# Turned tiles through DRAM in one transfer each way, larger pieces, Wqkv in parts, and a new order: a stack of four graph layers

## The chip, the cores and the metric

The kernel runs on one core of a Trainium2 chip. That core has TensorE (PE, matrix products into PSUM banks), VectorE (DVE), ScalarE (ACT), GpSimd (POOL) and SyncE (SP, which here only issues transfers), and 16 DMA engines that all issuing queues share. The metric is the device time of one execution in microseconds (us); lower is better. Times are medians over several executions. The profile is of one more execution.

## The reference

64 graphs of 256 nodes with 256 features pass through four layers. Each layer is followed by a residual and a normalisation without weights. Cut to what matters:

```python
# layer 0: transformer block over allowed = adj | adj.T | eye
q, k, v = split(x @ Wqkv.T + bqkv)            # 8 heads of 32
attn = softmax(where(allowed, q * scale @ k.T, -inf))
x1 = layernorm(x + (attn @ v) @ Wo.T + bo)
y = layernorm(x1 + relu(x1 @ W1.T + b1) @ W2.T + b2)
x = norm(x + y)
# layers 1 and 2: graph attention
h = x @ W.T                                    # layer 2: x @ W, no bias
e = leaky_relu(f[:, None] + g[None, :])        # f = h @ a1, g = h @ a2
x = norm(x + softmax(where(adj > 0, e, -big)) @ h + bias)   # layer 2: elu
# layer 3: two relation convolutions with mask adj == 1
h = elu(x @ w_root + (mask.T @ x / deg) @ w_rel + b)        # twice
x = norm(x + h)
```

All of it is float32. The second relation (`adj == 1` and `adj != 1`) is always empty.

## The kernel before

Everything for one graph is held as tiles of 128 partitions: 256 nodes are `NB` = 2 blocks of 128 nodes, 256 features are `KB` = 2 blocks of 128 features. A graph goes through some 60 operations. A small planner, `Plan`, receives all operations of all 64 graphs (`plan.op`: engine, planned cost, tiles read and written), and `schedule` decides the order in which each engine gets them. It walks through planned time. On each engine it takes, of the first 40 waiting operations, the ready one with the smallest due date. A due date is an entry of the table `DUE` (one per kind of operation) plus the graph's entry in `LATER`. Tiles live in rings of fixed size (`RINGS`: four `T`, one `turned`, one `blocks`, eight PSUM banks and so on); an operation waits until a buffer of its ring is free. The planned time matters only for the order: on the chip each engine runs its list, and semaphores do the waiting. Many graphs are in flight at once. TensorE changes between full products ("full"), scores in four row strips ("row", `L852`), values in four column strips ("col", `L873` and `L878`), single-pass gathers ("one", `L1036`) and transposes ("bits", "turn", "spread"); the planner counts a cost for a change of mode.

A matrix product needs its left operand with features on partitions. Where an activation has nodes on partitions it must be turned. Five times per graph (ahead of the feed-forward, of both graph attentions and of both convolutions) `bounced` does this without TensorE, for all but the last `QUICK` = 5 graphs: VectorE transposes 32x32 blocks (`L730`), SyncE sends the result to a DRAM tile `rows` in four transfers (`L734`, one for each 32 partitions, pieces of 128 bytes), then reads it back as `T` in one (`L737`, 2 KB per partition). The last five graphs go through ScalarE and TensorE instead (`L720`, `L709`, `L712`). The graph attention needs the column f on all partitions: VectorE transposes it (`L927`), SyncE writes it to DRAM (`L930`, `row<-cols`) and reads it back to all partitions (`L932`, `pf<-row`); then VectorE adds g and the mask (`L962`), applies the slope (`L965`), ScalarE takes the exponent (`L967`) and TensorE multiplies (`bank<-h,e`, in `product`, `L758`). The input x is read in eight strided transfers of 32-column blocks (`L748`) and transposed on VectorE (`L751`). SyncE carries all of these in one queue, with the loads of adj, x, xr, the weights and the output; a transfer that waits for its source holds up all that stand behind it.

At the start, GpSimd issues the loads of the small rows and columns (biases, norm weights) in program order, ahead of the planned part, and SyncE loads the weights as planned operations; Wqkv is one transfer of 768 KB (`L603`). GpSimd also computes the reciprocal root for each normalisation (`L772` to `L775`) and adds residuals with accumulating transfers (`L694`).

Of the kernel before, what the change touches and what calls it, by code (L numbers as in the profile page):

```python
# [18 lines left out]
P = 128  # L19
# [8 lines left out]
SENT, BACK = 3.2, 5.5  # L28
SENT_ROW, BACK_ROW = 2.6, 4.0
# [8 lines left out]
WORTH = 0.0  # L38
DUE = [
    -174.49, -30.67, -218.4, -13.1, -273.08, -58.54, -61.59, 77.04, -149.86, 411.77, 271.23, -47, 251.55, 289.26, 409.16, 111.82, -128.45, 340.23, 45.84, 214.03,  # L40
    175.89, -1.19, 78.77, -279.42, -23.39, 48.71, -130.17, -271.08, 149.73, -13.73, -89.69, -232.88, 470.18, 336.16, 222.8, 97.87, -54.4, -162.22, 370.88, 259.56,
    78.73, 64.78, 119.93, 148.71, -8.47, 151.17, -563.4, 216.96, 420.85, 105.36, -12.18, -73.5, -248.72, -183.23, -128.19, -297.4, -582.46, -629.93, -428.77, -624.34,
    -537.46, -889.65, -508.26, -787.82, -567.19, -632.7, -195.48, -656.32, -574.02, -727.78, -913.06, -538.96, -358.22, -951.51, -201.95, -392.63, -228.91, -130.77, -538.26, -399.3,
    -375.81, -885.24, -308.54, -281.69, -300.68, -236.73, -468.35, -102.24, -553.09, -355.09, -301.16, -135.84, -203.16, -68.79, 262.12, -373.58, -588.44, -396.63, -287.4, -163.41,
    -84.14, -161.3, 55.46, -37.62, -225, -68.62, -53.45, -173.79, -244.33, -312.15, -25.06, -130.25, -229.38, -357.91, -210.44, -689.16, -856.94, -453.15, -790.88, -481.92,
    -836.21, -389.2, -777.71, -103.26, -3.29, -1145.93, -317.53, -276.38, -81.48, -574.66, -449.44, -205.39, -496.42, 24.49, -179.79, -136.43, -325.16, 317.31, -603.82, -343.72,
    -371.81, -548.18, -331.53, -31.09, -128.17, 130.86, 1.87, 511.93, 153.26, 401.39, 149.72, -317.69, -500.74, -300.47, -371.15, -311.4, -333.58, 113.13, -178.32, -161.32,
    -448.39, -246.01, -410.16, -80.08, 6.31, -309.66, 11.59, -465.92, -681.64, -971.69, -916.97, -1014.65, -1262.62, -1383.05, -948.84, -855.59, -947.76, -1379.9, -710.53, -943.35,
    -553.21, -1028.37, -899.15, -683.97, -671.33, -379.95, -374.5, -674.01, -484.29, -173.96, -190.22, 54.18, -383.06, 111.01, -316.54, -124.36, -70.55, -86.53, -531.14, 531.14,
    -183.27, 110.54, 117.46, 350.27, -72.47, 19.93, -141.94, 64.33, 75.75, -83.28, 27.66, 87.87, -121.34, -128.76, 173.68, 156.59, 237.41, -282.51, 244.56, 209.74,  # L50
    181.62, 154.65, 180.84, 257.31, 326.57, 204.39, -182.17, 95.7, -191.88, -185.24, -7.82, -360.89, -20.59, -54.79, -173.03, 30.75, 310.52, 55.03, -458.58, -368.62,
    -301.68, -425.9, -464.37, -637.73, -768.61, -334.28, -150.16, -409.84, -355.26, 122.24, -107.85, -228.07, 47.36, 408, -92.61, 15.96, 80.96, 138.89, 67.4, 142.09,
    158.28, 47.13, -505.17, -320.95, -173.93, 136.21, 121.43, -45.74, -24.76, 91.57, -290.1, 89.8, -77.57, -224.12, 192.91, -503.22, -155.9, -61.04, -122.6, -163.72,
    -107.28, -293.92, -129.55, -48.17, -73.67, -152.32, -47.67, -88.39, -67.35, -95.35, -1.39, -120.46, -71.97, -99.95, -99.2, -83.54, -273.5, -100.86, -98.97, -246.65,
    -114.52, -84.34, -84.04, 213.08, -101.14, 28.99, -107.58, -166.35, -71.43, -370.62, -85.77, -54.9, -39.02, -105.24, -132.96, -80, 5.5, -143.22, -204.86, -87.44,
    -263.61, -54.97, -36.69, -15.51, -150.63, -138.2, -82.22, -46.11, -96.06, -107.06, -98.34, 5.8, -77.33, -106.96, -77.26, -94.63, 22.37, 44.75, 10.33, 81.65,
    -68.87, -13.71, -8.74, 3.65, 15.2, 59.74, -109.39, -109.42, -109.88, -122.53, -153.4, 80.8, -115.07, -211.16, -102.09, 220.31, -109, -81.64, -158.53, -140.27,
    -107.57, -47.12, -22.07, -162.83, 48.73, 31.08, -70.41, 95.56, -407.18, -102.6, 47.72, 10.89, -50.86, -71.44, -51.48, -13.16, -277.35, -101.83, -6.3, -268.19,
    -222.87, -172.64, -189.41, -85.76, -139.13, -181.79, -197.93, -115.69, -157.05, -73.06, -49.75, -158.63, -59.31, -93.55, -49.94, -151.39, -107.24, -72.78, -174.55, -70.55,
    -115.83, -293.85, -133.83, -133.95, -53, -133.17, -282.53, -145.74, -78.83, -104.42, -92.18, -145.7, -18.49, -17.87, 15.35, 6.67, 13.62, 57.04, -67.96, -80.53,  # L60
    39.58, -194.32, -44.64, -60.96, 7.1, -78.89, -48.83, -228.02, -4.68, -206.89, -2.65, -161.5, -34.42, -254.75, -53.95, -243.38, -118.23, -87.33, -28.27, -75.81,
    -104.07, -131.73, -309.88, -25.6, -45.95, -54.93, -91.47, -65.34, -123.35, -297.34, -138.27, -184.68, -109.73, -213.04, -117.5, -106.99, -266.96, -100.44, -97.67, -251.87,
    -284.74, -134.37, -0.22, -92.93, -117.19, -149.69, -97.23, -240.05, -139.35, 23.43, -35.17, -258.95, -117.88, -48.18, 188.95, -46.24, -145.12, -208.04, -268.67, -473.43,
    -272.21, -243.87, -112.49, -128.6, -313.79, -205.48, -109.56, 37.28, 213.35, -231.44, -290.26, -289.71, -171.01, -132.76, -35.5, -66.35, -9.67, -136.84, 463.57, -61.18,
    184.12, -198.15, 1.05, -86.21, -198.53, 114.21, -45.3, 54.56, -158.67, 15.98, -107.93, -77.74, -220.68, -453.53, -169.7, -88.06, -73.23, 116.03, -78.79, -74.27,
    -101.78, -96.73, 110.02, -273.88, -179.48, 265.32, -56.81, -46.47, -337.24, 102.8, -39.43, -355.3, 48.47, -235.68, -149.28, -635.75, -184.62, -148.96, -91.93, -52.81,
    -4.66, -351.52, -80.82, -238.88, 120.91, 93.83, 36.33, -177.41, -8.05, -48.92, 237.79, 75.79, 57.38, 313.29, 416.04, -82.45, 107.24, 191.68, 210.97, 64.43,
    -95.28, 310.12, 119.46, 67.34, -56.8, 46.35, 349.66, -74.87, -121.91, 34.56, 85.3, -52.75, 171.82, -341.78, -100.06, 126.59, -3, -262.55, 252.68, -39.97,
    -34.25, 131.75, -115.25, -2.99, -197.27, 22.45, -320.1, -187.93, -292.11, -133.05, -160.27, -66.47, -287.97, -208.92, -255.29, -419.07, -250.78, -500.29, -419.05, -440.34,
    -214.95, -115.45, -269.74, -319.13, -164.13, 4.5, 312.76, 82.06, 197.79, -30.08, -107.1, -286.77, -202.4, -646.95, -623.59, -467.76, -559.5, -318.22, -579.06, -404.03,  # L70
    -240.35, -65.58, -45.1, -153.25, 0.49, -146.16, 126.66, -34.71, -1.62, -179.37, -139.47, 227.43, -132.26, -290.26, -155.39, -51.64, 302.94, 246.87, 140.96, 204.3,
    -104.02, 71.81, 8.99, -126.86, 146.56, 0.86, 224.19, -152.01, 446.31, 131.78, 368.32, 314, 696.06, 347.08, 48.35, 187.69, 15.42, 78.29, 465.97, 264.4,
    166.9, 290.74, 160.47, 408.01, 590.72, 239.64, 475.03, 380.34, 133.8, 687.34, 377.65, 308.54, 177.24, 65.33, 352.6, 314.21, 19.52, 347.97, 321.54, -336.83,
    3.98, -110.06, -47.03, -163.4, -245.48, -59.58, 115.24, 69.33, 372.47, -20.84, 150.47, 264.59, -12.21, 46.26, 54.33, -331.12, -185.97, 15, -146.62, -307.28,
    -254.98, -482.4, 152.73, -443.86, -412.27, -99.19, -430.71, -271.66, -293.58, -545.9, -437.17, -236.15, -421.41, -139.02, -460.75, -814, -498.15, -872.83, -740.21, -107.52,
    -228.09, -535.02, -395.02, -152.46, -87.71, 186.76, -37.36, 173.3, 81.12, 213.05, -123.34, 215.75, -164.1, 319.76, 149, -26.56, 205.77, -219.36, 37.38, -51.04,
    12.57, -45.81, -10.44, -181.5, -100.86, 192.74, -72.9, 46.38, 442.42, -123.26, -157.49, -248.77, -433.39, -229.01, -111.35, -158.81, -169, -125.94, -243.05, -250.7,
    -209.85, -296.59, -119.49, -584.47, -331.14, -426.1, -318.14, -619.25, -168.44, -92.39, -109.4, -4.46, -154.38, -381.47, -282.5, -508.95, -97.11, -110.59, -181.94, -319.69,
    -366.24, -15.54, -364.82, -456.16, -363.15, 9.73, -177.14, -241.89, -206.34, 62.66, -415.85, -255.33, 28.1, 30.17, -150.26, -285.39, -10.72, -64.69, -59.2, -351.31,
    -213.36, -348.36, -100.2, -532.45, -196.58, -289.33, -155.62, -288.87, -509.51, -208.57, -148.76, -328.27, -11.7, -356.16, -232.87, -88.94, -499.61, -524.58, -539.29, -354,  # L80
# [1269 lines left out]
```

## Time and profile before

| | us |
|---|---|
| median of 3 runs (lowest to highest) | 2803.42 (2802.26 to 2806.78) |
| the profiled execution, its time | 2808.35 |
| its span, first to last instruction | 2806.6 |
| TensorE busy | 2744.8 |
| VectorE busy | 2480.0 |
| ScalarE busy | 1580.3 |
| GpSimd busy | 851.8 |
| mean granted TensorE clock | 0.996 of full |

The page lists the engines' busy time, where the span is cut into 40 slices, the queues of the transfers, a chain of work followed back from the last instruction, and groups of instructions by source line. A float32 product appears as two records; the ends of matmul records are modelled, so that a busy TensorE can hide short waits. "PEld" are weight loads, which run beside products. A wait line names the waiting engine and line, whom it waited for, the total, how often, and the longest. "SPq" is SyncE's queue: the duration there is that of issuing a transfer, not of the transfer.

### The profile page before, as it was taken

To read this page: it belongs to the slowest core of one execution; us is meant where nothing else is said; L and a number is where in the kernel's file an instruction comes from. 1 tells how busy PE (TensorE), PEld (TensorE's weight loads), DVE (VectorE), ACT (ScalarE), POOL (GpSimd) and SP (SyncE) were. 2 spreads that over 40 slices of the span, in tenths; PEclk is the share of its full clock that TensorE was granted. 3 is DMA by queue.
4 is the path that set the end of the run, shared out by engine and by line. 5 is a ranking of instruction groups with operands and counts; after the bars stand their busy time and mean duration, and the time that the engine had idled before them with its cause. 6 is when DMAs were issued, how large, how long until landed. Compare 5 with 4: busy or idle time off the path is not lost.

```text
span 2806.6 us, 50451 instructions
## 1 busy us (share of the span) xinstructions
PE 2744.8 (98%) x15790; PEld 2082.0 (74%) x15790; DVE 2480.0 (88%) x6527; ACT 1580.3 (56%) x3827; POOL 851.8 (30%) x1753
## 2 busy tenths in 40 slices
PE   6999999999999999999999999999999999999997
PEld 5787777777777777767777777777777777777784
DVE  5788989898898988989889899899899998889877
ACT  3555565554555645646556556556555565556576
POOL 3232233332323323323233223323332232333232
PEclk9999999999999999999999999999999999999999
DMA  8455665655656656565665655766566655664221
GB/s 193 98 110 109 127 136 111 133 124 109 131 113 137 124 113 128 113 133 118 123 126 118 133 119 112 142 120 130 109 128 132 122 121 115 130 141 100 55 43 32
DMA packets 960073, 330.62 MB, mean 118 GB/s; under 512 B 780184, under 2 KB 913304, under 8 KB 959800
## 3 DMA queue, kind: packets, MB, share of 16 engines
q1 hardware_dynamic: 915240, 276.32, 44.5%
q0 software_dynamic: 44560, 51.01, 12.2%
q8 instruction: 128, 2.10, 0.3%
q14 instruction: 145, 1.19, 0.1%
HBM read 183.12 MB, written 94.23 MB: 99 GB/s over the span
## 4 chain that ended last, share of the span: by engine, by line
PE 65%; DVE 18%; DMA 8%; SPq 3%; ACT 3%; issue 2%; POOL 1%; DVEq 0%; POOLq 0%; ACTq 0%
PE bank L758 55%; DMA rows<-turned 3%; PE bank L852 3%; PE bank L878 3%; PE bank L1036 3%; SPq L734 2%; DMA o<-X 2%; PE bank L873 2%; DVE turned L730 2%; DVE p L860 2%; DMA pf<-row 1%; DVE inv L884 1%; DVE st L767 1%; DVE X L689 1%; DVE lo L1024 1%
## 5 line engine op out<-in xcount | busy, mean ns | idle before, releaser
L772 POOL TENSOR_SCALAR rstd<-mv 128x2 f32<-128x2 f32 x384 | 102.0, 266 | 1434.4 <-DVE mv L769 1098.2
L758 PE MATMUL bank<-cw,T 128*128 128x512 f32 x1024 | 471.0, 595 | 1.5 <-DMA T<-rows 0.8
L779 ACT ACTIVATE X<-X,rstd 128x256 f32<-128x256 f32 x640 | 349.1, 596 | 214.9 <-POOL rstd L775 207.4
L758 PE MATMUL bank<-T,w 128*128 128x256 f32 x2048 | 464.4, 380 | 0.8 <-DMA T<-rows 0.6
L758 PE MATMUL bank<-w,hid 128*128 128x256 f32 x2048 | 460.6, 380 | 0.0
L758 PEld LDWEIGHTS bank<-w,hid 128*128 128x128 f32 x2048 | 387.4, 190 | 62.2 <-issue 10.7
L758 PEld LDWEIGHTS bank<-T,w 128*128 128x128 f32 x2048 | 385.2, 190 | 61.4 <-issue 9.0
L858 ACT ACTIVATE p<-bank 128x512 f32<-128x512 f32 x512 | 300.1, 598 | 100.0 <-PE bank L852 99.6
L860 DVE TENSOR_TENSOR p<-p,am 128x512 f32<-128x512 f32 x512 | 332.2, 677 | 14.2 <-ACT p L858 12.7
L758 PEld LDWEIGHTS bank<-cw,T 128*128 128x128 f32 x1024 | 188.8, 190 | 180.1 <-issue 162.7
L773 POOL TENSOR_TENSOR rstd<-rstd,neghalf 128x2 f32<-128x2 f32 x384 | 301.6, 785 | 32.1
L913 ACT ACTIVATE hid<-bank,col_b 128x256 f32<-128x256 f32 x512 | 215.8, 471 | 137.7 <-PE bank L758 136.6
L758 PE MATMUL bank<-h,e 128*128 128x259 f32 x1024 | 251.2, 386 | 10.4 <-ACT e L967 10.3
L758 PE MATMUL bank<-xT,wqkv 128*128 128x256 f32 x1024 | 245.2, 386 | 7.8 <-DMA wqkv<-in_WqkvT_dram 7.1
L758 PE MATMUL bank<-gw,T 128*128 128x258 f32 x1024 | 246.8, 382 | 1.3 <-DVE X L896 1.1
L758 PEld LDWEIGHTS bank<-h,e 128*128 128x128 f32 x1024 | 192.3, 191 | 72.8 <-issue 22.4
L884 DVE RECIPROCAL inv<-bank 128x256 f32<-128x256 f32 x128 | 221.3, 1739 | 25.9 <-PE bank L878 25.7
L767 DVE BATCH_NORM_STATS2 st<-X 128x6 f32<-128x256 f32 x640 | 236.3, 410 | 2.0
L758 PEld LDWEIGHTS bank<-xT,wqkv 128*128 128x128 f32 x1024 | 193.7, 192 | 48.7 <-issue 20.7
L730 DVE STREAM_TRANSPOSE turned<-X 128x512 f32<-128x512 f32 x236 | 165.3, 700 | 65.5 <-DMA rows<-turned 52.2
L758 PEld LDWEIGHTS bank<-gw,T 128*128 128x128 f32 x1024 | 191.3, 190 | 34.6 <-issue 5.5
L1023 ACT CAST hi<-bank 128x256 fp32r<-128x256 f32 x256 | 94.5, 370 | 211.0 <-PE bank L758 210.6
(129 smaller groups left out, 4684.5 us busy)
## 6 DMA issues: line engine op xcount, KB each, us to landing
rows<-turned SPq DMA_DIRECT2D x1180, 64.0 KB
T<-rows SPq DMA_DIRECT2D x295, 256.0 KB
adj<-in_adj_dram SPq DMA_DIRECT2D x128, 256.0 KB
blocks<-in_x_dram SPq DMA_DIRECT2D x512, 32.0 KB
x<-in_x_dram SPq DMA_DIRECT2D x64, 256.0 KB
xr<-in_x_dram SPq DMA_DIRECT2D x64, 256.0 KB
xr<-row_ln_b POOLq DMA_DIRECT2D x64, 256.0 KB, 4.7
x<-row_bo POOLq DMA_DIRECT2D x64, 256.0 KB, 4.9
```

What stands on the lines that cost most here:

```text
L730: dve(0.63, lambda: nc.vector.transpose(turned().rearrange("p b q n -> p (b q n)"), xt().rearrange("p i (k b c) -> p b (i k) c", k=KB, b=4 ...
L758: nc.tensor.matmul(dst, lhsT=lhs(c), rhs=rhs(c), start=(c == 0), stop=(c == n - 1))
L767: nc.vector.bn_stats(stat()[:, i, :], y()[:, i, :])
L772: nc.gpsimd.tensor_scalar(rstd()[:, 0, :], mv()[:, :, 1], 1.0, EPS, op0=ALU.mult, op1=ALU.add)
L773: nc.gpsimd.tensor_tensor(rstd()[:, 0, :], rstd()[:, 0, :], neghalf[:, 0:NB], op=ALU.pow)
L779: nc.scalar.activation(y()[:, i, :], y()[:, i, :], AF.Identity, bias=rstd()[:, 1, i : i + 1], scale=rstd()[:, 0, i : i + 1])
L852: nc.tensor.matmul(s[r]()[:, hg, :], lhsT=qk()[f, KB + hg, kt * P : (kt + 1) * P], rhs=qk()[f, hg, :], start=True, stop=True)
L858: act(0.58, lambda pr=pr, k=k, sr=s[r]: nc.scalar.activation(pr(), sr(), AF.Exp, accum_out=seen_sum[:, k : k + 1]), [s[r]], [pr])
L860: dve(0.60, lambda pr=pr, kt=kt: nc.vector.tensor_tensor(pr(), pr(), am()[:, kt, None, :].to_broadcast([P, KB, N]), op=ALU.mult), [pr, am] ...
L884: dve(1.62, lambda hg=hg, pc=pc: nc.vector.reciprocal(inv()[:, hg, :], pc()[:, 1, :]), [pc], [(inv, hg)])
L913: act(0.36, lambda f=f, k=k, ph=ph: nc.scalar.activation(hid()[:, f + k, :], ph()[:, k, :], AF.Relu, bias=b1[:, f + k : f + k + 1]), [ph, ...
L1023: act(0.27, lambda i=i, po=po: nc.scalar.copy(hi()[:, i, 0:D], po()[:, D:]), [po], [(hi, i)])
```

## The change

Six parts.

Turned tiles: `turned` gets the layout `[P, KB, 4 * NB * 32]` in which node m of block 0 and node m of block 1 stand side by side. One transfer writes it to `rows` (pieces of 1 KB), one reads it back (pieces of 256 bytes). `T` then holds node m of block i at column 2m + i, so that a product that wants one block takes every second column: the operand of TensorE has a step of two words, and so has the output of VectorE's transpose.

```diff
-                turned, rows, xT = new("turned", [P, 4, NB * KB, 32]), new("rows", [P, NB * KB, 4, 32]), new("T", [P, NB * KB, P])
-                dve(0.63, lambda: nc.vector.transpose(turned().rearrange("p b q n -> p (b q n)"),
-                                                      xt().rearrange("p i (k b c) -> p b (i k) c", k=KB, b=4)),
+                turned, rows, xT = new("turned", [P, KB, 4 * NB * 32]), new("rows", [KB, P, 4 * NB * 32]), new("T", [P, KB, NB * P])
+                x = NB * 32
+                dve(0.63, lambda: nc.vector.transpose(turned().rearrange("p k (b n i) -> p (k b) i n", b=4, i=NB),
+                                                      xt().rearrange("p i (j c) -> p j i c", c=32)),
                     [xt], [turned], "uses")
+                op("SP", 0.5, lambda: nc.sync.dma_start(rows().rearrange("k p x -> p k x"), turned()), [turned], [rows],
+                   lag=SENT, size=0.9)
+                def back():
+                    r = rows()
+                    nc.sync.dma_start(xT().rearrange("p k (a x) -> p (k a) x", a=4),
+                                      bass.AP(tensor=r.tensor, offset=r.offset, ap=[[x, P], [32 * 4 * x, KB * 4], [1, x]]))
+                op("SP", 1.0, back, [rows], [xT], lag=BACK, size=1.1)
+                return xT, lambda kb, i: xT()[:, kb].rearrange("p (m i) -> p i m", i=NB) if i is None else xT()[:, kb, i::NB]
-                for a in range(4):
-                    op("SP", 0.62, lambda a=a: nc.sync.dma_start(
-                        rows().rearrange("(c b) q a n -> c (b q) a n", b=4)[:, :, a, :],
-                        turned()[32 * a : 32 * a + 32].rearrange("c b q n -> c (b q) n")), [turned], [(rows, a)], lag=SENT)
-                op("SP", 0.43, lambda: nc.sync.dma_start(xT().rearrange("p q n -> p (q n)"), rows().rearrange("p q a n -> p (q a n)")),
-                   [rows], [xT], lag=BACK)
-                return xT, lambda kb, i: xT()[:, kb::KB, :] if i is None else xT()[:, KB * i + kb, :]
```

Input blocks: four transfers of 64 columns each instead of eight of 32, so pieces of 256 bytes instead of 128. The features of a partition change by this, and Wqkv's rows with them.

```diff
                 for a in range(4):
-                    for kb in range(KB):
-                        f = kb * P + 32 * a
-                        op("SP", 0.51, lambda a=a, kb=kb, f=f: nc.sync.dma_start(
-                            blocks()[32 * a : 32 * a + 32, kb], x_in[g, :, f : f + 32].rearrange("(m r) c -> r m c", r=32)),
-                           [], [(blocks, 4 * kb + a)])
+                    f = a * KB * 32
+                    op("SP", 0.53, lambda a=a, f=f: nc.sync.dma_start(
+                        blocks()[32 * a : 32 * a + 32], x_in[g, :, f : f + KB * 32].rearrange("(m r) c -> r m c", r=32)),
+                       [], [(blocks, a)], lag=2.2 if g < 3 else LOADED, size=0.25)
```

Wqkv: twelve transfers of 64 KB on ScalarE's queue, four for each of queries, keys and values. A product waits for its own third.

```diff
-            load(c_wqkv, wqkv, "WqkvT")
-            load(c_wo, wo, "WoT")
+            for part in range(3):
+                for a in range(4):
+                    plan.op("ACT", 0.5, lambda a=a, cut=slice(part * D, (part + 1) * D): nc.scalar.dma_start(
+                        wqkv[32 * a : 32 * a + 32, :, cut],
+                        t["WqkvT"][a * KB * 32 : (a + 1) * KB * 32, cut].rearrange("(k c) n -> c k n", c=32)),
+                        0, [], [(c_wqkv, (part, a))], size=0.25, lag=2.2)
+            load(c_wo, wo, t["WoT"])
```

Small constants: their loads on GpSimd become planned operations (`for w, (_, size, issues) in zip(small_tiles, loads): ... plan.op("POOL", 0.75, issue, ...)`), the two additions that prepare `bq` and `b2` too, and operations that read a constant name it.

Planner: transfers get a size, and share one planned bus; lags, costs and mode costs have new values; TensorE may hold for an operation that becomes ready within `HOLD`.

```diff
-SENT, BACK = 3.2, 5.5
-SENT_ROW, BACK_ROW = 2.6, 4.0
+LOADED = 3.2
+SENT, BACK = 1.4, 2.2
+SENT_ROW, BACK_ROW = 1.7, 3.2
-WORTH = 0.0
+WORTH, HOLD, WAIT = 158.14, 0.22, 23878.4
-    ENTER = {"full": 0.0, "row": 0.22, "col": 0.14, "one": 0.1, "turn": 0.22, "spread": 0.11, "bits": 0.01}
-    LEAVE = {None: 0.0, "row": 0.21, "col": 0.21, "one": 0.01, "turn": 0.01, "spread": 0.02, "bits": 0.07}
+    ENTER = {"full": 0.0, "row": 0.213, "col": 0.148, "one": 0.0, "turn": 0.0, "spread": 0.0, "bits": 0.0}
+    LEAVE = {None: 0.0, "full": 0.0, "row": 0.2, "col": 0.2, "one": 0.0, "turn": 0.0, "spread": 0.0, "bits": 0.057}
...
-                seen = end + (o.lag or self.LAG[e])
+                seen = end
+                if o.size:
+                    bus = seen = max(bus, end) + o.size
+                seen += o.lag or self.LAG[e]
```

Order: the tables `DUE` and `LATER` (some 870 and 64 numbers) are replaced as a whole, so every engine's list is a new one.

## Prediction

> **What bounds the kernel now.** I read the page's busy shares first, then TensorE's waits, then the timelines of the start and of one stall, then the DMA issues.
>
> The busy shares (part 1 of the page):
>
> ```profile
> span 2806.6 us, 50451 instructions
> ## 1 busy us (share of the span) xinstructions
> PE 2744.8 (98%) x15790; PEld 2082.0 (74%) x15790; DVE 2480.0 (88%) x6527; ACT 1580.3 (56%) x3827; POOL 851.8 (30%) x1753
> ```
>
> TensorE is the bound: it is idle for 2806.6 - 2744.8 = 61.8 us. Busy ends are modelled, so I worked out from the starts in the trace what TensorE must do. Two starts of full matmul records stand 0.216 us apart at 256 columns, 0.218 at 258 and 259, 0.429 at 512 (a float32 product is two records). Tiled ones (scores, values) go four at a time, 0.217 per four; a gather record takes about 0.11. With the counts of the groups: 6144 x 0.216 + 2048 x 0.218 + 1024 x 0.429 + 5120 / 4 x 0.217 + 1024 x 0.11 + 32 for the transposes and small products = 2635 us. A change of array mode costs more: in medians, 0.20 us into the scores and 0.21 out, 0.12 into the values and 0.22 out, 0.04 into or out of a gather, 0.06 after the mask transposes. Over the 715 stretches of one mode that is 79 us. So 2714 of 2806.6 us is work in order. The other 93: 10.6 ahead of the first matmul, 13 after the last product, about 70 of stalls and slow clock between.
>
> TensorE's waits (line, whom it waited for, us in total, times, longest):
>
> ```profile
> PE bank L796 <- DVE ident_b L417: 10.6, 1, 10.6
> PE bank L758 <- ACT e L967: 10.3, 9, 1.9
> PE bank L758 <- DMA wqkv<-in_WqkvT_dram: 7.1, 1, 7.1
> PE bank L1036 <- DVE lo L1024: 5.2, 7, 2.0
> ...
> PE bank L758 <- DMA T<-rows: 1.4, 3, 0.6
> ```
>
> Two things stand out: the start, with Wqkv, and the exponents of the graph attention. The transfers that the change's name speaks of, the turned tiles, are waited for 1.4 us in all. The start in TensorE's timeline (start, duration, what):
>
> ```profile
> 10.61 0.58 PE L796 MATMUL bank<-ident_b,bits 128*128 128x128 bf16 x4 [10.61 <-DVE ident_b L417]
> 18.29 6.69 PE L758 MATMUL bank<-xT,wqkv 128*128 128x256 f32 x16 [7.09 <-DMA wqkv<-in_WqkvT_dram]
> ```
>
> Sixteen records took 6.69 us; 16 x 0.216 is 3.5, so this stretch ran at about half speed. By my sums the stalls are about 23 us up to 100 us (the 7.1 and this slow clock in them), 7 in the last 100, and about 45 between. The largest come once in four graphs; one is at 887.8 us. SyncE's queue ahead of it:
>
> ```profile
> 876.52 3.64 SPq L734 DMA_DIRECT2D rows<-turned  x4
> 880.26 0.56 SPq L930 DMA_DIRECT2D row<-cols  x1
> ```
>
> And the chain that ended last, in the same stretch:
>
> ```profile
> 880.86 4.15 DMA pf<-row
> 885.01 0.03 issue
> 885.03 0.88 DVE e L962 x2
> ```
>
> The row's source, the transposed columns, was ready at about 878.0. Its transfer stood behind four transfers of one turned tile. So pf landed at 885.0, the exponent ran at 887.15, and TensorE lost some 2 us.
>
> **What the skill says.** "SBUF — State Buffer", Specifications (TRN2): a line is 16 bytes, and full bandwidth needs at least two accesses to a line. A step of two float32 words gives exactly two. The new T is read by TensorE with that step, and VectorE writes the turned tile with it. No operand of the kernel before has this step, so no run here shows it free. The ScalarE copy at L720, which reads with a step of 128 bytes, takes 1101 ns against 580 for the one at L712 (one reads SBUF, the other PSUM, so this is only a hint of what a bad step costs).
> "TensorE: Matmul & The Clock Gate", "Wait — 56ns, not 53.3ns?": N / 2.4 GHz + 2.5 ns. With 2 x 256 passes that is 215.8 ns; the trace's 216 agrees.
> "DMA: Bandwidth & Descriptors", "Issuing engines are not separate DMA queues": another issuer only saves issue time, since the engines are shared. The DMA share is 0.97 of full from 10 to 18 us, at 282 GB/s, so at the start the order of the bytes counts.
>
> **The change, part by part.**
>
> *Turned tiles.* Before, SyncE's issues (min/median/max ns):
>
> ```profile
> L734 SPq DMA_DIRECT2D rows<-turned x1180: 549/627/2317, 55.4 to 2675.6; - x197
> L737 SPq DMA_DIRECT2D T<-rows x295: 319/339/1145, 63.8 to 2677.9; - x148
> ```
>
> A tile costs 4 x 0.627 + 0.339 = 2.85 us of SyncE. After: one send of 256 pieces (an adj load with 256 pieces takes 0.40) and one readback of 1024 pieces, which the trace doesn't show. Its bounds are 0.34 (as now) and 2.5 (as the four sends, 2048 pieces). A line through 0.34 at 128 pieces and 0.63 at 512 gives 0.3 + 0.00075 per piece, some 1.0; I take that. So 1.4 us a tile, and 295 x 1.45 = 428 us of SyncE is freed. Latency now, in medians from the trace: 2.6 us from first to last send, 2.8 until the readback is issued, 2.4 to its last packet: 7.8. After: 0.4 + 2.8 + (2.4 + 0.7 for the longer issue + 0.5 for smaller pieces, an estimate) = 6.8. TensorE waits 1.4 us for T in all, so this second is worth under 1.4 us. The gain is in what stands behind the sends.
>
> *DMA time.* 735 thousand packets of 128 bytes at 14 ns and 37.8 thousand of 2 KB at 106 ns go: 14.3 ms over 16 engines. 75.5 thousand of 1 KB at 55 ns and 367.6 thousand of 256 bytes come. The last lie between 14 and 55 ns; by bytes, between these two points, 20. Sum 11.5 ms: 6 points of share less. At 55 ns it would be 24.4 ms, and the share would go from 57% to 79%.
>
> *Input blocks.* 512 issues of a median 0.45 us become 256 with the same number of pieces each: 115 us of SyncE freed, 128-byte pieces become 256.
>
> *Wqkv and the small constants.* SyncE gave 2.1 us to Wqkv at 6.08, and it landed 12.1 us later. Now ScalarE's queue, empty before 4.85 us, issues twelve parts from about 0.7, at 0.5 each; a product waits for the four of its own third. In the list of ScalarE the keys' third is complete with the seventh part, the queries' with the eighth, the values' with the last. ScalarE's first reader comes after them, at about 12 x 0.5 + 0.7 = 6.7, plus a table load of 1.28: before the first bank is full, so hidden; were the products ready sooner, it would cost up to 1 us. The eighth part is issued at about 4.5; a landing takes some 3 us, as for the rows. Two thirds, blocks and first adj are 1 MB, with 0.3 MB of others between; at 270 GB/s that is 5 us from about 2, the same. So the first product starts near 8 (not before 6, hardly after 12) instead of 18.3: 10.3 us. Then scores, exponents and masks take 10.8 us on ScalarE and VectorE as now (26.6 to 37.4). W1 and W2 stand behind on SyncE: 3.7 MB are to land before the small products with W1 at about 18 us, at 270 GB/s 14 us plus latency, just in time. POOL issues the constants in a new order, none is needed sooner than now, and the bias copy bq comes with the fourth. I take 10 us for the start, 5 to 14 as bounds.
>
> *The order.* TensorE's list has the same matmuls. Scores stand in 101 stretches instead of 123, gathers in 160 instead of 131, values 64 in both, but values are followed by a full product 61 times (28 before) where scores followed 16 times. With the medians above: 78 us against 79. Nothing is gained there. What can go is the 45 us of stalls. The planner's lags and sizes change, the send's from 3.2 us to 0.9 + 1.4 behind its issue and the row's return to 3.65 behind a 0.5 us issue; 4.15 together is what the trace shows for pf<-row (the line above). An order made with lags near the trace's holds fewer late operands, and the row transfer, when a send stands ahead of it, waits 0.4 us and not 3.6. Bounds: below nothing (a new order can stall in new places), at most 45. I take 25: the 10.3 us of exponents with what modelled ends hide of them, the waits on lo and hi (5.2 + 4.0), and half of the rest. VectorE's work is the same; if its 295 transposes (700 ns) stay at 700, it is busy 2480 of some 2770 us, and covered. If they took twice that, 206 us more would make VectorE 97% busy.
>
> *End.* From the last gather (2793.3 us) to the end the chain is exponent, normalisation and write, 13 us, the same after: 0. The 7 us of stalls there are QUICK's graphs, which don't use the bounce; I leave them.
>
> Sum: 10 + 25 = 35. The profiled execution took 2808.35, span and 1.75 around it; that gives 2773. The median of the runs, 2803.42, lies 5 below: 2768.
>
> **Rivals.** *Nearly all stalls go* (0.10): 2803 - 10 - 45 = 2748, with more of the start 2740; I take 2745. For it: work in order is 2714, and start and end cannot fall below about 8 + 13. Against: VectorE at 90% leaves little slack.
> *Only the start* (0.16): the sends were hidden anyway (1.4 us of waits), and the new order stalls as often as the old. 10 to 17 us, about 2790.
> *No change* (0.05): the DMA engines, at 0.87 of full from 24 to 60 us, are the bound there, and what the start gains is waited for at W1 and the first tiles: 2803.
> *Slower* (0.08): TensorE pays for the step of two words when it reads T. 2048 records read it as the moving operand, 2048 as weights. From 35 / 2048 = 17 ns more per moving record (8% of 216) the gain is gone; at twice the time 2048 x 0.216 = 442 us are lost. Weight loads have 190 ns in a slot of 216, so a tenth more is free for the 1024 of the graph attention, and twice costs 1024 x 0.16 = 164 us. A mild case gives 2850. For it: nothing here shows such a read. Against: two accesses per line, as the skill has it.
>
> **How the numbers follow.** The likeliest (0.61) is the sum, 2768, own range 2750 to 2787. Faster: 0.61 + 0.10 + 0.16 = 0.87; within 0.2% 0.05; slower 0.08 (0.2%, some 5.6 us, is about what a measurement tells from no change). From 2742 to 2800 lie the likeliest, the start alone and half of the best: 0.61 + 0.16 + 0.05 = 0.82.
>
> **What would show it.** The first product near 8 us and no wait for Wqkv; fewer waits on the exponents, and none of 2 us behind sends of a turned tile; readback issues near 1 us; records of T at 216 and 429 ns from start to start and transposes at 700 ns; 128-byte packets gone. I am wrong if T's records are further apart, if packets of 256 bytes take over 30 ns, or if stalls of 45 us stand in new places.

## The result, and the profile after

The changed kernel takes 2787.85 us (median, 2785.47 to 2791.18), the kernel before 2805.09 on the same chip: a ratio of 0.994, 95% interval 0.9923 to 0.9958. It is faster by 17 us; the forecast was 35. The profiled execution took 2788.03 us; its span is 20.3 us shorter than before's 2806.6.

The span and the busy shares of the changed kernel (part 1 of its page):

```profile
span 2786.3 us, 48831 instructions
...
PE 2749.3 (99%) x15790; PEld 2092.4 (75%) x15790; DVE 2498.9 (90%) x6527; ACT 1588.5 (57%) x3827; POOL 819.9 (29%) x1753
```

TensorE is idle for 37.0 us, where it was 61.8. But it is busy for 4.5 us longer on the same 15790 records. TensorE's waits (line, whom it waited for, us in total, times, longest):

```profile
PE bank L679 <- DMA blocks<-in_x_dram: 6.4, 1, 6.4
PE bank L824 <- DVE ident_b L427: 5.6, 1, 5.6
PE bank L786 <- ACT e L997: 3.6, 11, 0.7
...
PE bank L786 <- DMA T<-rows: 0.4, 2, 0.2
```

The waits on the exponents fell from 10.3 to 3.6 us, and none is over 0.7. The waits on `lo` and `hi`, 9.2 us before, are 1.1. (`hi` and `lo` are the two parts into which a convolution's product is split for the gathers; ScalarE makes the first, VectorE the second.) A new one stands first: L679, the 16 small products on W1. The view puts it down to a transfer of input blocks, but these are no operand of L679, and none of those under way landed before 26.4 us, after the products had begun. The last packet of W1 ended at 25.0 us, and in a run below with W1 loaded first the wait is gone. So it is W1 that is waited for. The start, in TensorE's timeline:

```profile
9.20 5.98 PE L786 MATMUL bank<-xT,wqkv 128*128 128x256 f32 x16 [2.98 <-DMA cw<-in_w_root_dram]
...
26.02 6.95 PE L679 MATMUL bank<-spread_ln_b,w 128*128 128x1 f32 x32 [6.35 <-DMA blocks<-in_x_dram]
32.91 1.08 PE L903 MATMUL bank<-both,ones 128*32 128x256 f32 x8
```

The first product starts 9.1 us earlier, at 9.20 (the transfer named beside it is no operand of it either). Later TensorE waits 6.35 us for W1, takes 6.95 us for 32 tiny records (213 ns each; the granted clock was 0.50 from 26 to 33 us), and begins the first values at 32.91, where the kernel before had them at 35.9. SyncE's issues (min/median/max ns):

```profile
L758 SPq DMA_DIRECT2D rows<-turned x295: 354/360/907, 62.3 to 2721.8; - x148
L763 SPq DMA_DIRECT2D T<-rows x295: 354/360/1214, 65.2 to 2724.0; - x148
```

SyncE's issues fell from 1473 us in all to 626. From the end of VectorE's turn to the issue of the readback the mean went from 6.0 to 3.4 us. Last, the product that reads T as its moving operand, in the page's list of groups (busy us, mean ns), the kernel before and then the changed one:

```profile
L758 PE MATMUL bank<-T,w 128*128 128x256 f32 x2048 | 464.4, 380 | 0.8 <-DMA T<-rows 0.6
```

```profile
L786 PE MATMUL bank<-T,w 128*128 128x256 f32 x2048 | 500.7, 390 | 0.0
```

From start to start these records are 227 ns apart (median), where they were 216. All other products kept their distance to within 1 ns, those with T as weights too (217 and 429 ns).

By the prediction's own count the 20.3 us divide so: ahead of the first matmul 5.0 us less; from there to 100 us 0.7 more; stalls between 100 and 2700 us 44.9 before, 30.8 after, of which 1888 records x 10.9 ns = 20.6 are the slower reads of T and 10.2 are stalls; mode switches 1 less, the end 1 less.

### The profile page after: what moved, and what is told of

The parts are those of the page before. It is cut to its first block, busy times and chain, and to the rows that moved or that the text cites. A ratio compares the mean times of both kernels' runs of the same rounds, so it can differ in the third digit from the quotient of the medians.

```text
span 2786.3 us, 48831 instructions
## 1 busy us (share of the span) xinstructions
PE 2749.3 (99%) x15790; PEld 2092.4 (75%) x15790; DVE 2498.9 (90%) x6527; ACT 1588.5 (57%) x3827; POOL 819.9 (29%) x1753
## 3 DMA queue, kind: packets, MB, share of 16 engines
q1 hardware_dynamic: 566856, 275.46, 36.1%
## 4 chain that ended last, share of the span: by engine, by line
PE 90%; DVE 4%; DMA 3%; ACT 2%; issue 1%; POOL 0%; ACTq 0%; SPq 0%; POOLq 0%; DVEq 0%
PE bank L786 75%; PE bank L882 4%; PE bank L908 4%; PE bank L1066 4%; PE bank L903 2%; DMA rows<-turned 1%; DMA T<-rows 1%; PE bank L824 1%; DVE p L890 0%; DMA row<-cols 0%; DMA pf<-row 0%; DVE turned L755 0%; DVE e L992 0%; DVE e L995 0%; ACT X L807 0%
## 5 line engine op out<-in xcount | busy, mean ns | idle before, releaser
L786 PE MATMUL bank<-T,w 128*128 128x256 f32 x2048 | 500.7, 390 | 0.0
L786 PE MATMUL bank<-cw,T 128*128 128x512 f32 x1024 | 462.7, 593 | 1.0 <-DMA T<-rows 0.4
L786 PEld LDWEIGHTS bank<-T,w 128*128 128x128 f32 x2048 | 379.5, 188 | 91.7 <-issue 13.9
L786 PEld LDWEIGHTS bank<-cw,T 128*128 128x128 f32 x1024 | 198.2, 195 | 188.0 <-issue 177.0
L801 POOL TENSOR_TENSOR rstd<-rstd,neghalf 128x2 f32<-128x2 f32 x384 | 294.8, 768 | 32.2
L786 PE MATMUL bank<-h,e 128*128 128x259 f32 x1024 | 260.1, 383 | 3.7 <-ACT e L997 3.6
L786 PE MATMUL bank<-xT,wqkv 128*128 128x256 f32 x1024 | 260.5, 390 | 3.0 <-DMA cw<-in_w_root_dram 3.0
L1080 ACT ACTIVATE e<-o 128x512 f32<-128x512 f32 x128 | 80.6, 630 | 217.8 <-DVE o L1076 215.9
```

Of the source, the lines that this page charges most:

```text
L786: nc.tensor.matmul(dst, lhsT=lhs(c), rhs=rhs(c), start=(c == 0), stop=(c == n - 1))
L801: nc.gpsimd.tensor_tensor(rstd()[:, 0, :], rstd()[:, 0, :], neghalf[:, 0:NB], op=ALU.pow)
```

## The experiments

The kernel before took 2805.09 us beside the first four runs, 2811.6 and 2810.6 beside the next two groups, so the ratios are what compares. "Stalls" means the same count between 100 and 2700 us. The last column is the wait ahead of the turns, for the transfer that still reads the one `turned` tile. It is VectorE's but for 1.2 us in the changed order and 7.2 us in that order with the old transfers, where ScalarE turns tiles of the last graphs.

| kernel | ratio to before (95%) | span, us | stalls, us | wait for `rows<-turned`, us |
|---|---|---|---|---|
| before | 1 | 2806.6 | 44.9 | 56.5 |
| changed | 0.9940 (0.9923 to 0.9958) | 2786.3 | 30.8, with 20.6 of slower reads | 7.4 |
| changed, T read as it lies | 0.9886 (0.9871 to 0.9901) | 2771.7 | 17.8 | 8.6 |
| changed order, old transfers | 1.0823 (1.0806 to 1.0840) | 3030.4 | 260.2 | 216.4 |
| the same, second turned buffer | 1.0741 (1.0722 to 1.0761) | 3025.9 | 261.6 | none listed |
| old order, new row transfer, T read as it lies | 0.9881 (0.9866 to 0.9896) | 2772.8 | 12.7 | 1.3 |
| the same, send cut in four | 0.9906 (0.9892 to 0.9919) | 2781.7 | 20.5 | 20.2 |
| the same (one send), with blocks and Wqkv as changed | 0.9863 (0.9847 to 0.9879) | 2771.7 | 12.6 | none listed |
| before, blocks and Wqkv alone | 0.9941 (0.9928 to 0.9954) | 2791.5 | 32.0 | 42.6 |
| before, second turned buffer alone | 0.9892 (0.9878 to 0.9907) | 2777.5 | 15.8 | none listed |

### What the step of two words costs

The feed-forward can read T as it lies if the columns of `hid` may stand in pairs; the second product then takes the step, as weights:

```diff
-  lambda kb: x1T_at(kb, None), KB), [x1T, c_w1], [ph], [hid])
+  (lambda kb: x1T()[:, kb]) if g < B - QUICK else (lambda kb: x1T_at(kb, None)), KB), [x1T, c_w1], [ph], [hid])
...
-  product(po()[:, i, :], lambda c: lhs(c)[:, i * P : (i + 1) * P], rhs, n)
+  product(po()[:, i, :], lambda c: lhs(c)[:, i::NB] if turned else lhs(c)[:, i * P : (i + 1) * P], rhs, n)
```

> The changed kernel with the first feed-forward product reading T as it lies (256 adjacent words), the columns of hid then standing in pairs, and the second product picking its 128 weights out of hid at a step of two words. Everything else, the order included, stays. Theory (the step of the moving operand costs TensorE 11 ns a record on 1888 records, a step in the weights nothing): T,w records come back from 227 to 216 ns start to start, w,hid stays at 216 ns, and the kernel takes 21 us less than the changed one: about 2767 us, 0.986 to 0.987 of the kernel before. Rival 1 (the step costs the same as weights): w,hid goes to 227 ns and the time stays at 2788 us, 0.994. Rival 2 (the 11 ns come from row transfers that write into T while it is read, not from the step): T,w stays at 227 ns and the time at 2788 us.

It took 2773.58 us, 14 less than the changed kernel. The group of the same product, and of the one that now reads its weights at the step:

```profile
L786 PE MATMUL bank<-T,w 128*128 128x256 f32 x2048 | 480.9, 382 | 0.0
L786 PE MATMUL bank<-w,hid 128*128 128x256 f32 x2048 | 461.6, 379 | 1.3 <-ACT hid L943 1.3
```

Both stand at 216 ns from start to start. So the step costs as a moving operand and not as weights, and the transfers that write T meanwhile have no part in it. The gain is 14 us where 21 were expected: a TensorE that arrives earlier meets new waits, and the stalls are 17.8 us where 10.2 had been left (changed, then T as it lies):

```profile
PE bank L786 <- DMA T<-rows: 0.4, 2, 0.2
```

```profile
PE bank L786 <- DMA T<-rows: 3.4, 4, 1.8
PE bank L1066 <- DVE lo L1054: 2.3, 4, 1.0
```

The disputed cost by itself: products of two loaded tiles, nothing beside them.

```diff
+  pairs = moving[:, 0:256].rearrange("p (m i) -> p i m", i=2)
+  mm(weights[:, 0:P], moving[:, 0:256])     # contiguous
+  mm(weights[:, 0:P], pairs)                # the even words, then the odd ones
+  mm(weights[:, 0:P], moving[:, 0:1024:4])  # step 4; and 8
+  mm(weights[:, 0:512:4], moving[:, 0:256]) # weights at step 4; and 2
```

> Leaves the whole network out: products of 128 weights by 256 moving columns (f32) of two loaded tiles, 32 products for each way of reading, twice, with no transfer beside them. Theory (the step itself costs): contiguous 216 ns a record and 216 for two pieces of 128; even words and then odd ones 227 ns; steps of four and eight words more than that, perhaps 250 ns and up; weights at steps of two and four words 216 ns. Rival (transfers beside it cost): every way of reading 216 ns.

Stretches of it, in this order: contiguous, even and odd words, step four, weights at step two, weights at step four. A line gives the stretch and its length in us, then the busy us and the records of TensorE, then those of its weight loads. The third stretch is twice as long:

```profile
36.00:48.00 12.00, 12.00 (x58) 10.58 (x57) 0.00 (x0) 0.00 (x0) 1.00 0.00 0
64.00:76.00 12.00, 12.00 (x54) 9.95 (x53) 0.00 (x0) 0.00 (x0) 1.00 0.00 0
93.00:117.00 24.00, 24.00 (x54) 11.01 (x53) 0.00 (x0) 0.00 (x0) 1.00 0.00 0
151.00:163.00 12.00, 12.00 (x57) 10.92 (x57) 0.00 (x0) 0.00 (x0) 1.00 0.00 0
165.00:177.00 12.00, 12.00 (x53) 12.00 (x53) 0.00 (x0) 0.00 (x0) 1.00 0.01 1
```

Mean from start to start: contiguous 215.8 ns (two pieces of 128 the same), step of two 226.7, four 450.8, eight 460.0; weights at two 216.1, at four 233.3. The step itself costs, as the theory had it; that four words would double the time was not expected. As weights a step of two costs nothing (216.1 ns), and at four the weight loads are busy all the time (12.00 of 12.00).

### The transfer and the order, each alone

Old transfers in the changed order: one planned send issues the four old transfers, one planned readback the old one.

```diff
-  op("SP", 0.5, lambda: nc.sync.dma_start(rows().rearrange("k p x -> p k x"), turned()), [turned], [rows], lag=SENT, size=0.9)
+  def send():
+      for a in range(4):
+          nc.sync.dma_start(rows().rearrange("(c b) q a n -> c (b q) a n", b=4)[:, :, a, :],
+                            turned()[32 * a : 32 * a + 32].rearrange("c b q n -> c (b q) n"))
+  op("SP", 0.5, send, [turned], [rows], lag=SENT, size=0.9)
```

> The changed kernel and its order with the old transfer alone put back: a planned send issues the four old transfers one after another, the readback is one of 2 KB a partition, and T is read in pieces of 128 adjacent words. Theory (both the transfer and the order shorten the stalls; the step goes away with the old layout): T,w at 216 ns gives back 21 us, but SyncE has 295 times 3 more issues, about 428 us in all, so row transfers land later than the order assumes by 1 to 2 us and TensorE's waits behind them (on exponents, T and turned) rise from about 9 us to 25 to 50 us: between 2785 and 2810 us, 0.993 to 1.002. Rival (the order alone removed the stalls; one transfer in place of four is worth nothing): stalls stay at 9 us and the time falls to about 2767 us, 0.987.

3034.06 us: both theories are far off. T's records stand at 216 ns again, but TensorE waits everywhere:

```profile
PE bank L785 <- DMA T<-rows: 74.6, 61, 3.0
PE bank L1065 <- DVE hi L1058: 38.0, 22, 2.5
PE bank L785 <- ACT e L996: 26.8, 42, 2.7
PE bank L1065 <- DVE lo L1053: 18.5, 23, 1.5
```

So the changed order cannot do without the changed transfer: T lands too late for it 61 times, and the wait ahead of the turns is 216.4 us. Now the other way round, the new transfer in the old order. Of the four planned sends the first issues the one transfer, the others nothing:

```diff
   for a in range(4):
-      op("SP", 0.62, lambda a=a: nc.sync.dma_start(
-          rows().rearrange("(c b) q a n -> c (b q) a n", b=4)[:, :, a, :],
-          turned()[32 * a : 32 * a + 32].rearrange("c b q n -> c (b q) n")), [turned], [(rows, a)], lag=SENT)
+      op("SP", 0.62, lambda a=a: a == 0 and nc.sync.dma_start(rows().rearrange("k p x -> p k x"), turned()),
+         [turned], [(rows, a)], lag=SENT)
```

> The kernel before and its order with the new transfer alone put in: the first of the four planned sends issues the one new transfer, the other three issue nothing, the readback is in 256-byte pieces, and the first feed-forward product reads T as it lies. Theory (the transfers' time on SyncE makes part of the 45 us of stalls): SyncE's issue time falls by about 400 us, the stalls on exponents late behind row transfers and on row values fall by 10 to 20 us, no step is paid: 2783 to 2795 us, 0.992 to 0.996. Rival (the order makes the stalls): within 3 us of the kernel before, 2802 to 2808 us, 0.999 to 1.001.

2772.55 us: 32.5 less than before, more than the theory gave and 15 less than the changed kernel. With T read as it lies in both, the two orders end level (0.9881 and 0.9886), though this one has none of the edits to the start. TensorE's wait on exponents in this run:

```profile
PE bank L763 <- ACT e L972: 3.4, 4, 1.4
```

Is it the number of issues or the size of the packets? The same with the send cut in four by partitions, which keeps every packet:

```diff
-  lambda a=a: a == 0 and nc.sync.dma_start(rows().rearrange("k p x -> p k x"), turned()),
+  lambda a=a: nc.sync.dma_start(rows().rearrange("k p x -> p k x")[32 * a : 32 * a + 32], turned()[32 * a : 32 * a + 32]),
```

> The kernel before and its order with the new transfer and contiguous reading, as in the run of before's order above (2772.6 us), but the send cut into four issues of 32 partitions each: the same packets, 885 more issues. Theory (the issues on SyncE made the stalls): at 360 ns or more each, SyncE has 319 us or more of issues again, and 20 to 34 us of stalls come back: 2792 to 2806 us, 0.995 to 1.000. Rival (the 128-byte packets of the old send made them, being more work for the DMA engines): it stays within 3 us of 2772.6 us, 0.987 to 0.990.

2783.47 us, 0.9906 (its interval still touches that of the single send): neither. The issues came back (1198 us of SyncE in all, against 778), but only 8 of the 32 us of stalls with them. Each of these issues was shorter than an old one, too (min/median/max ns):

```profile
L735 SPq DMA_DIRECT2D rows<-turned x1180: 302/428/2248, 56.4 to 2650.3; - x197
```

From first to last of the four it is a median of 1.8 us, with the old ones 2.6. What goes with the stalls in the table is not the number of issues but the wait ahead of the turns.

### How the old sends reached TensorE

There is one `turned` tile. VectorE's next turn may not write it until the transfer has read it. VectorE's wait ahead of its turns in the kernel before (in total, times, longest), and two of these in its timeline:

```profile
DVE turned L730 <- DMA rows<-turned: 56.5, 48, 4.6
```

```profile
515.88 0.71 DVE L730 STREAM_TRANSPOSE turned<-X 128x512 f32<-128x512 f32 x1 [4.47 <-DMA rows<-turned]
1206.48 0.71 DVE L730 STREAM_TRANSPOSE turned<-X 128x512 f32<-128x512 f32 x1 [3.82 <-DMA rows<-turned]
```

In the first, SyncE issued four sends from 509.49 on; VectorE stood still for 4.47 us until they were through. From there it worked almost without a pause up to the `lo` that it ended at 522.09, and for this TensorE had waited:

```profile
522.14 0.38 PE L1036 MATMUL bank<-lo,rel 128*128 128x256 f32 x1 [0.96 <-DVE lo L1024]
```

The test takes the wait's reason away and leaves the transfers and the order as they were (the change to the guard values is not shown):

```diff
+  if name == "turned":
+      turns[0] += 1
+      i = turns[0] % 2
   return pools["work"].tile(shape, dtype, tag=f"{name}{i}", name=name)
```

> The kernel before with a second buffer for the turned tile, used in turn; transfers and order stay. To make room the guard values that are looked at after the last graph are kept for the last 32 graphs only, which leaves that part of the guard out. Theory (VectorE's next turn waits for the four old sends to have read the one turned tile, 56.5 us in all, and that is how the sends reach TensorE): the wait falls under 10 us, TensorE's 45 us of stalls to 15 to 25 us, 2776 to 2790 us, 0.990 to 0.995. Rival (as in the prediction: the rows of the graph attention stand behind four sends in SyncE's queue): VectorE's wait goes but the exponents stay late, 2797 to 2806 us, 0.997 to 1.000.

2779.37 us, 0.9892, as the theory had it: the buffer alone gives nearly what the new transfer gives. (The shorter guard is not the reason: in the last run of this part it comes with the second buffer and nothing is gained.) VectorE's wait is gone, TensorE's stalls are 15.8 us, and the exponents, behind four sends as ever, are waited for half as long:

```profile
PE bank L766 <- ACT e L975: 4.7, 9, 1.0
```

SyncE's issues are unchanged (1479 us). So in this order the sends cost what they did mostly by holding the tile that VectorE was to write.

In the changed order with the old transfers, the same buffer:

> The changed order with the old transfers (3034 us above, VectorE waiting 216 us for the turned tile), and a second buffer for the turned tile as in the run beside it, with the same part of the guard left out. Theory (the wait for the one turned tile carries most of the 250 us): 2800 to 2880 us, 0.998 to 1.027. Rival (the later landing of T and of the rows carries it): over 2960 us, 1.055 and up.

3018.42 us; the rival holds. The 216 us of waits for the tile are gone, the ratio falls only from 1.0823 to 1.0741, and TensorE's stalls in the profiled executions are the same 261 us, with another name:

```profile
PE bank L793 <- DMA T<-rows: 155.4, 110, 3.6
```

There TensorE waits most for the landing of T. And in the version that was left with 8.6 us of this wait, the changed kernel with T read as it lies:

> The changed kernel with T read as it lies in the feed-forward product (2773.6 us above) and a second buffer for the turned tile, the same part of the guard left out. VectorE still waits 8.6 us for that tile and TensorE has some 16 us of stalls between 100 and 2700 us. Theory (the new send still holds VectorE up): 2 to 6 us less, 2767 to 2772 us. Rival (these waits are beside the path): within 1.5 us of 2773.6 us.

2775.10 us at a slower before: 0.9877 (0.9863 to 0.9892) against 0.9886, no difference. The short waits that are left cost nothing that can be measured.

### The start

W1's loads ahead in SyncE's list:

```diff
+  order = [o for o in order if o not in w1_loads]
+  k = next(i for i, o in enumerate(order) if o.engine == "SP" and o in setup_ops)
+  order[k:k] = w1_loads
```

> The changed kernel with the four loads of W1 moved ahead of those of conv weights, W2 and x in SyncE's list; nothing else moves. Theory (W1 landing at 25.0 us holds the small products and the values behind them): some 1.4 MB no longer stand ahead of W1's last part, it lands near 18 us, TensorE's 6.4 us wait on it goes and the first values start near 25 us in place of 32.9: 6 to 8 us off the changed kernel's 2788 us, 2780 to 2782 us, 0.991 to 0.992 of the kernel before. Rival (what now lands later, the second graph's blocks, x or W2, makes the same wait further on): 2785 to 2790 us.

The ratio is 0.9954 (0.9938 to 0.9970), no better than the changed kernel's. The first values did start earlier, by 8.6 us (TensorE's timeline):

```profile
19.33 3.63 PE L683 MATMUL bank<-spread_ln_b,w 128*128 128x1 f32 x32
24.30 1.15 PE L907 MATMUL bank<-both,ones 128*32 128x256 f32 x6 [1.34 <-DVE both L898]
...
57.30 1.98 PE L790 MATMUL bank<-xT,wqkv 128*128 128x256 f32 x4 [2.19 <-DVE xT L782]
```

But by 65 us the lead is 0.2 us, and the first graph's result is written at the same time as without it (243.7 and 243.8 us). It went into waits for later input blocks, those of the third and fourth graph, in VectorE's timeline:

```profile
42.89 0.71 DVE L782 STREAM_TRANSPOSE xT<-blocks 128x512 f32<-128x512 f32 x1 [2.34 <-DMA blocks<-in_x_dram]
56.45 0.71 DVE L782 STREAM_TRANSPOSE xT<-blocks 128x512 f32<-128x512 f32 x1 [3.59 <-DMA blocks<-in_x_dram]
```

SyncE issued the blocks of the second line only from 52.79 us, behind four transfers `gw<-ga` that kept its queue from 48.47 to 52.69.

The small products moved behind the first values, loads as they were:

```diff
+  order = [o for o in order if o not in w1_uses]
+  k = order.index(values) + 1
+  order[k:k] = [o for o in w1_uses if o.engine == "PE"]
...
```

> The changed kernel with the 16 small products on W1 and the three VectorE operations that follow from them moved behind the first graph's values; the loads stay. Theory: the values start at about 25 us, when their operands are there, and the small products then find W1 landed: 5 to 8 us off, 2780 to 2783 us. Rival (TensorE at half clock or waiting further on takes the time back): 2785 to 2790 us.

0.9954 (0.9941 to 0.9966): the rival again; the values start at 23.97 us and the lead is gone by 60 us. Until the inputs of the first four graphs have landed, an early product was only early. What holds these back is not shown: in the first 60 us the DMA engines of the changed kernel are busy for 0.81 of the time at 198 GB/s, and SyncE's queue has its part, as the four `gw<-ga` show; no run parts the two.

The other two transfer edits alone, on the kernel before (blocks in four, Wqkv in twelve parts on ScalarE's queue):

```diff
-  load(c_wqkv, wqkv, "WqkvT")
+  for part in range(3):
+      for a in range(4):
+          nc.scalar.dma_start(wqkv[32 * a : 32 * a + 32, :, cut], ...)
...
-  for kb in range(KB): ... nc.sync.dma_start(blocks()[32 * a : 32 * a + 32, kb], ...)
+  nc.sync.dma_start(blocks()[32 * a : 32 * a + 32], x_in[g, :, f : f + KB * 32].rearrange("(m r) c -> r m c", r=32))
```

> The kernel before and its order with only the input blocks in four and Wqkv in twelve parts on ScalarE's queue; row transfers, T and reading stay. Theory (both only move waits about while the start is held by what all loads take together; 115 us of issues fewer on SyncE spare a few stalls): 2 to 6 us less than before, 0.998 to 0.9993. Rival (the prediction's: an earlier first product counts in full, 10 us, and the freed queue adds): 2790 to 2796 us, 0.995 to 0.9965.

0.9941 (0.9928 to 0.9954), 15.1 us of span: more than my theory gave, as much as the whole change (0.9940), but not where the rival said. The first product came at 16.84 us, only 1.4 earlier, though Wqkv's parts were all issued by 9 us: VectorE waited for the first graph's last input blocks.

```profile
16.07 0.71 DVE L758 STREAM_TRANSPOSE xT<-blocks 128x512 f32<-128x512 f32 x1 [8.11 <-DMA blocks<-in_x_dram]
```

So the old order never had an early first product, and this run doesn't tell what one is worth there. The first graph's result comes only 2.9 us earlier; the other 12 come over the whole run, as stalls fall from 44.9 to 32.0 and VectorE's wait for the turned tile from 56.5 to 42.6 us. SyncE has 146 us of issues less, so sends start sooner (0.10 us after the turn in the mean, 0.32 before).

All three transfer edits on the old order, with T read as it lies:

> The kernel before and its order with the new transfer, contiguous reading, and the other two transfer edits of the change as well: Wqkv in twelve parts on ScalarE's queue, input blocks in four. Theory (before's order has its small products where W1 has landed, so an earlier first product counts in full): the first product moves from 18.3 to about 10 to 12 us, and the kernel takes 5 to 8 us less than with the row transfer alone: 2764 to 2768 us, 0.985 to 0.987. Rival (the next load to land, W1 or adj of the first graphs, takes the time back as in the changed kernel): 2770 to 2775 us.

0.9863 (0.9847 to 0.9879), the lowest ratio and faster than both kernels, but its interval meets that of the row transfer alone (0.9866 to 0.9896). The first product did not move to 10 or 12 us here either; it came at 17.33. The 15 us of the start edits and the 34 of the row transfer do not add up, 35 together: they remove the same waits. And the changed kernel with T read as it lies, which has these three edits in the new order and the constants loaded in the new way, ends with the same span, 2771.7 us (0.9886, 0.9871 to 0.9901): order, planner and constants together show no gain. None of the three was run alone.

## Why the prediction was right or wrong

**Direction and bound: right.** Faster, TensorE still the bound, mode switches worth 1 us less as foretold. The size was twice too large. The step that failed is the one that put TensorE's reads of T with a step of two words at nothing: they cost 20.6 us, and this sign of being wrong, "T's records are further apart", came true. The other two terms were off as well, the start too large by 6 us and the stalls too small by 10. That these nearly cancel is luck, and so is the place in the range (2742 to 2800), just outside the likeliest case's own (2750 to 2787). The number is also that of the rival "only the start" (10 to 17 us), but not its mechanism: the start gave 4 us, and the stalls did go.

**The start, 10 us: wrong size.** The first product came at 9.20 us, close to the 8 foretold. What failed here is "3.7 MB are to land before the small products with W1 at about 18 us ... just in time": W1's last packet ended at 25.0. By then 5.3 MB had been moved, 1.2 of them in GpSimd's queue, which carries the constants; the mean was 213 GB/s, though 281 from 10 to 18 us. Yet W1 loaded earlier was worth nothing, so the deeper fault is to have counted the first product in full: in the runs above a lead lasted only until the inputs of the first four graphs had landed. The start gave 4 us. The rival "no change" had named this mechanism ("what the start gains is waited for at W1 and the first tiles").

**The stalls, 25 of 45 us: the transfer was the cause, by another path, and the term was too small.** Without the slower reads 10.2 us of stalls are left, so 35 went. The chain shown was real, a row transfer behind four sends, but it was taken for the main one. VectorE's wait for the one turned tile (56.5 us in 48 turns) was not in the sum; the prediction had read the 1.4 us that TensorE waits for T and not what VectorE waits for. A second buffer alone removes 29 of the 45 us. The edits to blocks and Wqkv alone remove 13; these gains overlap.

**"An order made with lags near the trace's holds fewer late operands": not shown.** The old order with the new transfer has 12.7 us of stalls, the new one with T read as it lies 17.8.

**The step of two words, 0: wrong.** The likeliest case took the Trainium skill's two accesses to a line ("SBUF — State Buffer", Specifications (TRN2)) as free. Measured, 226.7 ns against 215.8, 5% more; one access to a line, at a step of four, 450.8. The page's rule separates cheap from dear, but two are not full speed here. The slower rival had the mechanism and its break-even, 17 ns; the truth is 11 ns on 1888 records (the last five graphs do not read T so, which its 2048 leaves out), 20.6 us, and 14 of them come back when T is read as it lies. The step in weights was rightly put at nothing.

**The rest.** Readback issue 0.36 us, not 1.0: 1024 pieces cost no more than 256. Packets of 256 bytes 18 ns, estimated 20; the share of SyncE's queue fell from 44.5% to 36.1%, 8 points, where 6 were estimated. Transposes stay at 700 ns with a step-of-two write. The end gave 1 us, not 0.

With the measured terms (start, stalls, mode switches with the end, slower reads of T) the sum is 4 + 35 + 2 - 20.6 = 20 of span, where it was 10 + 25.

## What to carry to other kernels

When a transfer is slow to be sent, ask first which engine must write its source next. Here a second buffer of 2 KB a partition, with everything still queued behind the sends, did nearly the work of a new layout (0.9892 against 0.9881). If a layout has to put a step of two float32 words somewhere, try it on the weights, or let it pass through to a tile that is read as weights next. Gains that each remove the same waits do not add, and an order of work has its worth only together with its transfers: test each of them with the other one old.

## What the runs showed of the hardware that I had not expected

- A float32 moving operand of 256 columns: 215.8 ns contiguous or in two pieces of 128, 226.7 at a step of two words, 450.8 at four, 460.0 at eight. The weights of the same product: 216.1 at two, 233.3 at four.
- SyncE's issue time did not follow the number of pieces: a median of 360 ns for 256 pieces of 1 KB and for 1024 of 256 bytes, but 627 for each of four sends of 512 pieces of 128 bytes in a row, and 428 for four of 64 pieces of 1 KB in a row.
- After TensorE had waited 6.35 us for W1, 32 one-column records took 6.95 us (213 ns apart, granted clock 0.50). In the run with W1's loads first there was no such wait, and they took 3.63 us (112 ns apart, clock 1.00); there the clock was 0.50 later, from 23.2 to 30.1 us.
